# The first layer norm taken through a Toeplitz convolution: scaled transposed input, 1/std at the gate, mean and shift as a rank product

## The chip, the cores and the metric

The kernel runs on one core of a Trainium2 chip. The metric is the device time of one execution in microseconds (us), the median over several runs. A profiled execution on the same chip gives the trace from which all shares, durations and waits below are read.

Engines by the names of the profile: PE is TensorE (matmuls; PEld its weight loads), DVE is VectorE, ACT is ScalarE, POOL is GpSimd, SP is SyncE, whose queue issues nearly all DMAs here.

## The reference

One block of a network over x of shape (4, 1024, 2048) in fp32: an adaptive layer norm, a long convolution along the last axis, a gate, then a second adaptive layer norm, a feed-forward layer with a sum of low-rank updates, and a second gate.

```python
mod = (silu(c) @ wmod).reshape(4, 6, 1, 2048)
sa, ca, ga, sb, cb, gb = (mod[:, i] for i in range(6))
ga = (2 * (ga >= 0) - 1) * maximum(abs(ga), 0.25)        # gb likewise
h = layernorm(x) * (1 + ca) + sa
K = s4_kernel(...)                                        # 2048 taps, from small inputs
x = x + ga * (irfft(rfft(h, 4096) * rfft(K, 4096))[..., :2048] + D * h)
h = layernorm(x) * (1 + cb) + sb
x = x + gb * (h @ W.T + bias + sum_e w_e * (h @ A_e.T) @ Bf_e.T)
```

`layernorm` takes mean and variance over the 2048 columns. The convolution is causal and runs along the same 2048 columns that the norm runs over, with one kernel K for all rows. Both weights `ca`, `sa` depend on the batch entry (four of them) and the column.

## The kernel before, in words

**Tiles and stages.** The 4096 rows are 32 tiles of 128 rows, eight tiles to a batch entry. There are three stages. In the start, the modulation vectors come from 16 MB sections of `wmod` (tiles `wm`, 1 MB each; matmuls `modps`, line 317) and the convolution's taps are computed and laid out as Toeplitz blocks in a high and a low fp16 half (`kh`, `kl`, lines 233 to 287). Then comes the convolution of the 32 row tiles, and with it, as filler, the merging of the low-rank updates into W (`merge`, matmuls `lps`, line 486) and the three remaining sections of `wmod`. Last comes the feed-forward stage, 16 units of 256 rows by 2 column halves (`ffn_unit`, line 750), by a seven-product scheme.

**One row tile of the convolution.** `conv_load` (line 560) brings in x. `stats` (536) takes mean and variance with four `bn_stats` and one `bn_aggr`, and 1/std by a square root on ACT with a Newton step on DVE (`rstd`, 64). `normalize` (551) writes `n` = (x - mean)/std on DVE. `conv_prep` (565) transposes n, 16 blocks of 128x128, on PE into PSUM (`tp`, line 578), scales by 1 + ca and adds sa on ACT (line 582; both stand per partition once n is transposed), adds neighbouring column blocks to `sm` (590), and splits blocks and sums into fp16 high and low halves `hc`, `hs` (592, 593). `conv_mm` (596) multiplies these with the Toeplitz blocks: three families of matmuls, two column halves each, three products (high·high, high·low, low·high) per block pair, at line 614, into PSUM tiles `ya` and `yb`; the result is multiplied by the gate `gat` (633, 640), x is added and the row sums are kept (641). `conv_post` (654) stores the new x to `x1d` in HBM and takes the second norm's mean and 1/std into `ln2`.

**Scales.** The fp16 halves need bounded values. `fold_scale` (364) multiplies ca and sa by a power of two per batch entry, from the largest ca and sa over all partitions (`allmax`, line 58, one all-reduce over partitions on POOL); `gate_tile` (665) takes the scale out again.

**The two early rows.** Rows 0 and 1 (`EARLY`) are convolved in the start, before sa and the gate are known: their prep uses 1 + ca alone with a scale of its own (`early_scale`, 381). The convolution of the shift sa is made once with small matmuls (`shift_conv`, 390), stored to HBM, read back on all partitions and added (`shift_add`, 410); gate and x follow in `conv_late` (645).

**What sets the order.** The kernel's text says in which order work is issued; a scheduler then fixes every engine's queue before the run, by that order and by what is ready, as far as buffers allow. Each queue is worked through strictly in that order. Inside `conv_mm`, ten points (`tick`) call up the work of other rows after the strings of `PLAN` (line 812): P the second norm of the row before, N a piece of the next row's prep, S a piece of the filler, T the statistics of the row after next, F the first piece of that row's prep, L pieces of the feed-forward's left operands (last two rows). x has four buffers; PSUM has five banks for products (`acc`), two for transposes (`tps`), one for the modulation.

Of the kernel before, what the change touches and what calls it, by code (L numbers as in the profile page):

```python
# [26 lines left out]
NB = 4  # L27
# [7 lines left out]
class Net:  # L35
# [28 lines left out]
    def rstd(self, pool, var, out, n, name, scale=1.0):  # L64

        v = self.nc.vector
        ve = pool.tile([P, n], F32, tag=name + "_v", name=name + "_v")
        t = pool.tile([P, n], F32, tag=name + "_t", name=name + "_t")
        v.tensor_scalar(ve, var, 0.25 * scale, 0.25e-5, MUL, ADD)
        self.nc.scalar.activation(t, ve, AF.Sqrt)  # L70
        v.reciprocal(out, t)
        v.scalar_tensor_tensor(t, ve, out, t, MUL, ADD)
        v.reciprocal(out, t)
# [216 lines left out]
    def prep_mod(self, pool):  # L290
        nc, v = self.nc, self.nc.vector
        self.small = pool.tile([P, 265], F32, tag="small", name="small")
        nc.sync.dma_start(out=self.small, in_=self.io["small"])
        c = self.small[:, 201:265].rearrange("p (b j) -> p b j", j=16)
        th = pool.tile([P, NB, 16], F32, tag="mth", name="mth")
# [13 lines left out]
    def mod_load(self, pool, sec, j):  # L309
        w = pool.tile([P, D], F32, tag="wm", name="wm")  # L310
        src = self.io["wmod"].rearrange("(p j) n -> p j n", j=16)
        self.lastw = self.nc.sync.dma_start(out=w, in_=src[:, j, ds(sec * D, D)])
        return w
# [24 lines left out]
    def mod_gate(self, pool, name, bias=None):  # L338
# [10 lines left out]
        if bias is not None:  # L349
            bt = pool.tile([P, 512], F32, tag="mg2", name="mg2")  # L350
# [13 lines left out]
    def fold_scale(self, pool, mul, add, name, winv=None):  # L364
# [9 lines left out]
        self.hs, inv = s, _ = self.pow2(self.cst, self.allmax(pool, m, NB, name), NB, name)  # L374
# [6 lines left out]
    def early_scale(self, pool):  # L381
        v = self.nc.vector
        m = pool.tile([P, 1], F32, tag="esm", name="esm")
        v.tensor_reduce(m, self.ca[:, :, 0], AX.X, ALU.max, apply_absolute_value=True)
        v.tensor_scalar(m, m, LNMAX, None, MUL)
        self.es, self.einv = self.pow2(self.cst, self.allmax(pool, m, 1, "es"), 1, "es")
        self.cae = self.kpool.tile([P, NC], F32, tag="cae", name="cae")
        v.tensor_scalar(self.cae, self.ca[:, :, 0], self.es, None, MUL)

    def shift_conv(self, pool):  # L390

        nc, v = self.nc, self.nc.vector
        sa = pool.tile([P, NC], F32, tag="sae", name="sae")
        v.tensor_scalar(sa, self.sa[:, :, 0], self.es, self.hinv[:, 0:1], MUL, MUL)
        ps = self.tps.tile([P, NC], F32, tag="t", name="gsp")
        for m in range(NC):
            nc.tensor.matmul(
                ps[:, m:NC], self.kb[:, ds(P * m, P)], sa[:, 0 : NC - m],
                start=(m == 0), stop=(m == NC - 1), skip_group_check=True,
            )  # L400
        col = pool.tile([P, NC], F32, tag="gsc", name="gsc")
        v.tensor_copy(col, ps)
        pt = self.tps.tile([NC, P], F32, tag="t", name="gst")
        nc.tensor.transpose(pt, col, self.ident)
        row = pool.tile([NC, P], F32, tag="gsr", name="gsr")
        v.tensor_copy(row, pt)
        self.gsd = self.dram.tile([NC, P], F32, tag="gsd", name="gsd")
        nc.gpsimd.dma_start(out=self.gsd, in_=row)

    def shift_add(self, pool, ys):  # L410
        g = pool.tile([P, D], F32, tag="gat", name="gsb")
        self.nc.gpsimd.dma_start(out=g, in_=self.gsd.rearrange("c t -> (c t)").partition_broadcast(P))
        for y in ys:
            self.nc.vector.tensor_tensor(y, y, g, ADD)
# [121 lines left out]
    def stats(self, pl, x, tag):  # L536
        v = self.nc.vector
        st = pl["sm"].tile([P, 4, 6], F32, tag="st" + tag, name="st" + tag)
        for q in range(4):
            v.bn_stats(st[:, q], x[:, ds(512 * q, 512)])  # L540
        mv = pl["sm"].tile([P, 2], F32, tag="mv" + tag, name="mv" + tag)
        v.bn_aggr(mv, st)
        rs = pl["sm"].tile([P, 1], F32, tag="rs" + tag, name="rs" + tag)
        self.rstd(pl["sm"], mv[:, 1:2], rs, 1, "r" + tag)
        if tag in ACTNORM:
            mb = pl["sm"].tile([P, 1], F32, tag="mb" + tag, name="mb" + tag)
            v.scalar_tensor_tensor(mb, mv[:, 0:1], -1.0, rs, MUL, MUL)
            return mb, rs
        return mv, rs

    def normalize(self, pl, x, st, tag):
        n = pl["n"].tile([P, D], F32, tag="n", name="n" + tag)
        m, rs = st
        if tag in ACTNORM:
            self.nc.scalar.activation(n, x, AF.Identity, bias=m, scale=rs)
        else:
            self.nc.vector.tensor_scalar(n, x, m[:, 0:1], rs, SUB, MUL)
        return n

    def conv_load(self, pl, r):  # L560
        x = pl["x"].tile([P, D], F32, tag=f"x{r % 4}", name="x")
        self.nc.sync.dma_start(out=x, in_=self.io["x"][ds(P * r, P), :])
        return x

    def conv_prep(self, pl, r, x, st, out, shift=True):
        nc, v = self.nc, self.nc.vector
        b = r // 8
        n = self.normalize(pl, x, st, "1")
        yield

# [3 lines left out]
        for c0 in range(0, NC, 4):  # L574
            tp = self.tps.tile([P, 4, P], F32, tag="t", name="tp")
            t = pl["t"].tile([P, 4, P], F32, tag="t", name="t")
            for k in range(4):
                nc.tensor.transpose(tp[:, k], n[:, ds(P * (c0 + k), P)], self.ident)  # L578
            for k in range(4):
                c = c0 + k  # L580
                if shift:
                    nc.scalar.activation(  # L582
                        t[:, k], tp[:, k], AF.Identity,
                        bias=self.sa[:, c, b : b + 1], scale=self.ca[:, c, b : b + 1],
                    )
                else:
                    nc.scalar.activation(t[:, k], tp[:, k], AF.Copy, scale=self.cae[:, c : c + 1])
            tv = t.rearrange("p (i e) n -> p i e n", e=2)
            sm = pl["t"].tile([P, 2, P], F32, tag="sm", name="sm")
            v.tensor_tensor(sm, tv[:, :, 0, :], tv[:, :, 1, :], ADD)  # L590
            for (hi, lo), src, sl in ((hc, t, slice(c0, c0 + 4)), (hs, sm, slice(c0 // 2, c0 // 2 + 2))):
# [4 lines left out]
    def conv_mm(self, pl, hs, x, tick, early, pace):  # L596
# [4 lines left out]
        if not early:  # L601
            gv = self.gat.rearrange("p (j e t) -> p j e t", e=2, t=P)
        sums = pl["sm"].tile([P, 2], F32, tag="sums", name="sums")

        def family(ps, f, q, first):
            pf = ps.rearrange("p j t -> p (j t)")
            last = 4 * q + 3
            for i in range(last + 1):
                o = P * max(0, i - 4 * q)
                k0 = P * max(0, 4 * q - i)  # L610
                with pace(3 * (512 - o)):
                    for x, z in ((0, 0), (0, 1), (1, 0)):
# [5 lines left out]
                        first = False  # L618
                if i == 3 and q == 1:
                    tick()  # L620

        for q in range(2):
# [9 lines left out]
            if not early:  # L632
                v.tensor_tensor(yv[:, jj, 1, :], yv[:, jj, 1, :], gv[:, jj, 1, :], MUL)
# [5 lines left out]
            else:  # L639
                v.tensor_tensor(yv[:, jj, 0, :], pa, gv[:, jj, 0, :], MUL)  # L640
# [4 lines left out]
    def conv_late(self, x, y, sums, ratio):  # L645

        v = self.nc.vector
        for q in range(2):
            sl = ds(1024 * q, 1024)
            v.scalar_tensor_tensor(y[:, sl], y[:, sl], ratio, self.gat[:, sl], MUL, MUL)  # L650
# [3 lines left out]
    def conv_post(self, pl, r, x, y, sums):  # L654
        nc, v = self.nc, self.nc.vector
        STQ(nc).dma_start(out=self.x1d[r], in_=y)
        mn = pl["sm"].tile([P, 1], F32, tag="mn", name="mn")
        v.tensor_scalar(mn, sums[:, 0:1], sums[:, 1:2], -1.0 / D, ADD, MUL)
        sq = pl["sm"].tile([P, 1], F32, tag="sq", name="sq")
        nc.scalar.activation(x, y, AF.Square, bias=mn, accum_out=sq)  # L660
        rs = self.ln2[:, r, 1:2]
        self.rstd(pl["sm"], sq, rs, 1, "r2", 1.0 / D)
        v.tensor_tensor(self.ln2[:, r, 0:1], mn, rs, MUL)

    def gate_tile(self, pool, b):
# [3 lines left out]
        s = self.hinv[:, b : b + 1]  # L669
        if b == 0:  # L670
            for q in range(4):
# [3 lines left out]
                v.tensor_scalar(t[:, ds(512 * q, 512)], ps, s, self.kinv, MUL, MUL)  # L675
        else:
            nc.sync.dma_start(out=t, in_=self.gad[b].partition_broadcast(P))
            v.tensor_scalar(t, t, s, self.kinv, MUL, MUL)
# [133 lines left out]
PLAN = ("PNSL", "NL", "NSL", "NTL", "SL", "SL", "SL", "SL", "FSL", "SSL")  # L812
LPLAN = ("LL", "LL", "LL", "LL", "L", "0", "")
R0 = 5
WM, WMS = 3, 3
# [17 lines left out]
def net(ctx: ExitStack, tc: tile.TileContext, io):  # L833
# [5 lines left out]
    k.ln2 = k.const("ln2", [P, 32, 2])  # L839
    k.lfd = k.dram.tile([NU, 7, P, HC, 2, P], F16, tag="lfd", name="lfd")  # L840
# [10 lines left out]
    k.prep_mod(msm)  # L851

    def section(sec, pools):
# [5 lines left out]
        if sec == 0:  # L859
            k.sa = k.mod_column(msm, k.kpool, "sa", 0.0)  # L860
            k.hinv = k.fold_scale(msm, k.ca, k.sa, "fs1")
# [24 lines left out]
    for name, bufs in (("h", 2), ("n", 1), ("t", 2), ("y", EARLY), ("g", 1)):  # L886
        pl[name] = pool(left, "p1" + name, bufs)
    st = ExitStack()
    toe = k.toeplitz(pool(st, "st", 1, "right"))
    wms = pool(st, "wms", WMS, "right")  # L890
# [3 lines left out]
    xs, hs, sts, ys = {}, {}, {}, {}  # L894

    def prep(r, shift=True):
        return k.conv_prep(pl, r, xs[r], sts.pop(r), hs, shift)
# [4 lines left out]
    def load(r):  # L902
        if r < 4:
            with tc.issue_after(k.lastw.ins):
                xs[r] = k.conv_load(pl, r)
        else:
            xs[r] = k.conv_load(pl, r)

    def stats(r):
        sts[r] = k.stats(pl, xs[r], "1")  # L910

    n = 0
    for _ in section(1, (wms, wmp)):
# [6 lines left out]
    k.early_scale(msm)  # L920
    load(1)
    rows = (x for sec in (0, 2) for x in section(sec, (wms, wmp)))
    stats(0)
    take(prep(0, False), 9)
# [3 lines left out]
    take(prep(1, False), 9)  # L928
# [11 lines left out]
    def third():  # L940

        while not hasattr(k, "hinv"):
            yield
        k.shift_conv(msm)
        stats(2)
        yield from prep(2)

    ys[0] = k.conv_mm(pl, hs.pop(0), xs[0], lambda: None, True, pace)
    load(2)
    nxt = third()  # L950
    ys[1] = k.conv_mm(pl, hs.pop(1), xs[1], lambda: take(nxt, 1), True, pace)
# [3 lines left out]
    k.shift_add(pl["g"], [ys[r][0] for r in range(2)])  # L955
# [211 lines left out]
```

## Time and profile before

| what | value |
|---|---|
| median of 3 runs | 2142.18 us (2141.35 to 2144.37) |
| profiled execution, span | 2140.1 us, mean granted PE clock 0.988 |
| DMA | 484.11 MB, mean 226 GB/s; HBM read 326.94 MB, written 155.30 MB |
| first and last store of a finished convolution row | issued at 181.7 and 922.8 us |
| normalize (line 557, DVE) | 32 x 1340 ns |
| transposes of n (line 578, PE) | 512, mean 280 ns of one record |
| scale and shift (line 582, ACT) | 480 x 471 ns, from PSUM |
| split, high (592, ACT) and low (593, DVE), 128x512 | 128 x 640 ns and 128 x 684 ns |
| gate (633 and 640, DVE), 128x512 | 60 x 682 ns and 60 x 683 ns |
| POOL, whole run | 18 instructions, of which 5 all-reduces of 0.35 to 0.51 us |

The span is the time from the first to the last instruction of the one profiled execution; a stretch of it is named by its microseconds. A group's mean is the duration of one record, and records of one engine can overlap: matmuls follow each other faster than one of them takes from start to end. A row ends with the time that its engine sat idle just before the group, and with what ended most of that idle time.

### The profile page before, as it was taken

Reading aid. Unit: us, or ns where it says so; the run is one execution under the profiler, and the core shown is the slowest. Engines: PE = TensorE matmul, PEld = TensorE weight load, DVE = VectorE, ACT = ScalarE, POOL = GpSimd, SP = SyncE. Lnnn points to the kernel's source line nnn. Section 1 sums busy time; section 2 is a strip of 40 time slices with the busy share of each in tenths; the row PEclk is TensorE's granted clock in tenths of the full one; section 3 lists DMA queues with packets and bytes.
Section 4 is the critical chain, followed back from the end, with each engine's and each line's share of the span. In section 5 each row is a group of like instructions: output and inputs, shape, how many; then the busy total and the mean of one; then the engine's idle time right before and its main releaser. Section 6 shows DMA issues by size and latency. Waiting matters only on the chain.

```text
span 2140.1 us, 28438 instructions
## 1 busy us (share of the span) xinstructions
PE 2082.4 (97%) x11113; PEld 1026.1 (48%) x11113; DVE 1308.4 (61%) x2353; ACT 923.7 (43%) x1695; POOL 6.3 (0%) x18
## 2 busy tenths in 40 slices
PE   7898999999999999999999999999999999999998
PEld 2344455555555555554545545555444444444444
DVE  5439898898979999665565565575533323332323
ACT  1325876677767777745454555555200000000000
POOL 0000000000000000000000000000000000000000
PEclk7999999999999999999999999999999999999999
DMA  9977566787776554387564564564794645454542
GB/s 401 373 307 278 225 227 265 285 310 262 276 278 227 187 192 173 139 346 258 190 241 180 202 240 179 203 235 172 283 341 163 192 151 167 164 170 165 177 157 69
DMA packets 127236, 484.11 MB, mean 226 GB/s; under 512 B 13608, under 2 KB 13768, under 8 KB 95998
## 3 DMA queue, kind: packets, MB, share of 16 engines
q1 hardware_dynamic: 126192, 477.55, 61.4%
q10 hardware_dynamic: 526, 2.63, 0.4%
q8 instruction: 87, 1.43, 0.3%
q0 software_dynamic: 384, 2.11, 0.2%
q14 instruction: 47, 0.39, 0.0%
HBM read 326.94 MB, written 155.30 MB: 225 GB/s over the span
## 4 chain that ended last, share of the span: by engine, by line
PE 67%; DVE 18%; ACT 6%; DMA 5%; issue 2%; SPq 0%; ACTq 0%; POOL 0%; DVEq 0%; POOLq 0%
PE fZ L750 22%; PE fY L750 15%; PE fX L750 15%; PE ya L614 5%; PE yb L614 3%; PE tp L700 3%; DVE wch L514 2%; PE modps L317 2%; DVE st L540 2%; DVE hc L593 2%; DVE y L641 2%; ACT x L660 2%; DMA wcd<-wch 1%; ACT t L582 1%; PE lps L486 1%
## 5 line engine op out<-in xcount | busy, mean ns | idle before, releaser
L750 PEld LDWEIGHTS <-lf 128*128 128x128 f16 x5376 | 526.0, 98 | 620.9 <-issue 1.4
L750 PE MATMUL fZ<-w,lf 128*128 128x512 f16 x2304 | 513.6, 379 | 0.8 <-ACT p L758 0.8
L750 PE MATMUL fX<-w,lf 128*128 128x512 f16 x1536 | 342.8, 379 | 0.0
L750 PE MATMUL fY<-w,lf 128*128 128x512 f16 x1536 | 342.0, 379 | 0.0
L614 PEld LDWEIGHTS <-hc 128*128 128x128 f16 x2304 | 215.3, 98 | 204.6 <-issue 41.6
L768 DVE TENSOR_TENSOR xo<-xo,gb 128x512 f32<-128x512 f32 x128 | 87.8, 690 | 238.7 <-DMA xo<-x1d 227.2
L582 ACT ACTIVATE t<-tp,sa,ca 128x128 f32<-128x128 f32 x480 | 188.1, 471 | 21.6 <-PE tp L578 12.9
L614 PE MATMUL ya<-kh,hs 128*128 128x512 f16 (+3 forms) x768 | 193.7, 326 | 3.7 <-DVE kh L284 2.6
L614 PE MATMUL ya<-kh,hc 128*128 128x512 f16 (+3 forms) x768 | 192.7, 328 | 3.8 <-ACT qs L627 3.6
L614 PE MATMUL yb<-kh,hc 128*128 128x512 f16 (+3 forms) x768 | 192.2, 327 | 1.8 <-DVE y L640 1.4
L758 ACT COPY p<-fZ 128x512 f32<-128x512 f32 x64 | 37.2, 581 | 286.8 <-PE fZ L750 272.1
L614 PEld LDWEIGHTS <-hs 128*128 128x128 f16 x1152 | 105.9, 98 | 108.6 <-issue 28.4
L758 ACT COPY p<-fX 128x512 f32<-128x512 f32 x32 | 18.7, 585 | 316.3 <-PE fX L750 210.4
L702 ACT ACTIVATE gt<-tp,sb,cb 128x256 f32<-128x256 f32 x256 | 124.9, 576 | 60.8 <-PE tp L700 60.8
L317 PE MATMUL modps<-wm,sct 128*32 128x512 f32 x768 | 118.8, 662 | 14.1 <-DMA wm<-in_wmod 14.1
L614 PE MATMUL ya<-kl,hc 128*128 128x512 f16 (+3 forms) x384 | 125.8, 328 | 0.0
L614 PE MATMUL ya<-kl,hs 128*128 128x512 f16 (+3 forms) x384 | 125.1, 326 | 0.7 <-DVE kl L285 0.7
L614 PE MATMUL yb<-kl,hc 128*128 128x512 f16 (+3 forms) x384 | 125.6, 327 | 0.0
L773 DVE TENSOR_TENSOR fin<-fX,gb 128x512 f32<-128x512 f32 x32 | 22.1, 692 | 128.4 <-PE fX L750 128.3
L593 DVE TENSOR_TENSOR hc<-t,hc 128x512 f16<-128x512 f32 x128 | 87.5, 684 | 6.6 <-ACT hc L592 6.4
L486 PE MATMUL lps<-lbh,lac 128*128 128x512 f16 x256 | 86.3, 379 | 1.2 <-DVE we L488 1.2
L578 PE MATMUL tp<-ident,n 128*128 128x128 f32 x512 | 79.3, 280 | 8.1 <-ACT t L582 6.3
(264 smaller groups left out, 2228.0 us busy)
## 6 DMA issues: line engine op xcount, KB each, us to landing
wm<-in_wmod SPq DMA_DIRECT2D x96, 1024.0 KB
lfd<-lf SPq DMA_DIRECT2D x112, 512.0 KB
lf<-lfd SPq DMA_DIRECT2D x112, 512.0 KB
x<-in_x SPq DMA_DIRECT2D x32, 1024.0 KB
x1d<-y SPq DMA_DIRECT2D x32, 1024.0 KB
x<-x1d SPq DMA_DIRECT2D x32, 1024.0 KB
xo<-x1d SPq DMA_DIRECT2D x128, 256.0 KB
out<-xo SPq DMA_DIRECT2D x128, 256.0 KB
```

The lines of the kernel that those rows point to most:

```text
L317: self.last = self.nc.tensor.matmul(self.modps[32 * g : 32 * g + 32, :], self.sct[:, j].rearrange("p r b -> p (r b)"), w[:, ds(512 * g, 512)],
L486: nc.tensor.matmul(ps, la[:, x, k, h], y[:, k, osl], start=(n == 0), stop=(n == 5))
L514: v.tensor_tensor(hl[:, :, 1, :], tv, hl[:, :, 0, :], SUB)
L578: nc.tensor.transpose(tp[:, k], n[:, ds(P * (c0 + k), P)], self.ident)
L582: nc.scalar.activation(t[:, k], tp[:, k], AF.Identity, bias=self.sa[:, c, b : b + 1], scale=self.ca[:, c, b : b + 1],)
L593: v.tensor_tensor(lo[:, sl], src, hi[:, sl], SUB)
L614: nc.tensor.matmul(pf[:, o:512], h, self.kf[f][z][:, ds(k0, 512 - o)], start=first, stop=(i == last and (x, z) == (1, 0)), skip_group_chec ...
L700: nc.tensor.transpose(tp[:, c, r], xs[r][:, ds(P * (c0 + c), P)], self.ident)
L702: nc.scalar.activation(t[:, c0 + c], tp[:, c], AF.Identity, bias=self.sb[:, c0 + c, b : b + 1], scale=self.cb[:, c0 + c, b : b + 1],)
L750: nc.tensor.matmul(ps[name], lf[i][:, k, x, :], wc[i][k // 4][:, k % 4, y, :], start=(first and n == 0), stop=(n == 3 * HC - 1), skip_grou ...
L758: nc.scalar.copy(t, ps[name])
L768: v.tensor_tensor(x, x, self.gbias[:, h], ADD)
```

## The change

The norm is linear in x once mean and 1/std are known, and both are one number per row, while the convolution acts along the columns. The changed kernel uses that: with a row's mean m and standard deviation d, the convolution of (x - m)/d·(1 + ca) + sa is 1/d times [conv(x·(1 + ca)) - m·conv(1 + ca) + d·conv(sa)].

- **Input.** The host hands in x a second time, transposed by 128x128 blocks (`in_xT`, 1 MB per row tile). `conv_load` loads both. `normalize` and the 16 transposes per row are gone; `conv_prep` scales the transposed x in place on ACT by `cas` = (1 + ca)·s, now 8 blocks at a time, and sum and splits run on twice the width.
- **Scale.** The power of two s is made per row tile, from the largest of |m| + 46·d over the partitions and the largest |1 + ca| per batch entry (`scale_bound`, once): one all-reduce per row tile on POOL, with small operations on POOL (`g.`) and DVE around it.
- **Mean and shift.** `rank_rows` convolves -(1 + ca) and sa of all four batch entries once (8 vectors), splits them in three bf16 parts and stores them; `rank_load` brings them into `gm`, 72 of 128 partitions used, by 24 small DMAs on POOL. Each row's m·s and d·s are split in three bf16 parts as well, put into 18 columns of a 128x128 tile `spt`, transposed on PE (`svp`) and copied to bf16 (`sw`). One matmul of `sw` with `gm` per PSUM tile (`rank`) then adds mean and shift to the product.
- **Gate.** 1/std with the scale taken out (`rsx`, one number per row) is multiplied in at the gate, in a three-operand form.
- **Second norm.** `conv_post` keeps the sums of squares in `sqs` and makes 1/std for eight rows at once.
- **Order.** The prep of row r + 1 now starts and ends within row r's convolution (F is gone from `PLAN`); the transposed x has two buffers. In the start, `wm` takes turns over other free buffers: six at a time for the first section as before, five for the second and third.

The diff, cut to its core:

```diff
+    def scale_bound(self, pool):
+        m = pool.tile([P, NB], F32, tag="esm", name="esm")
+        v.tensor_reduce(m, self.ca.rearrange("p c b -> p b c"), AX.X, ALU.max, apply_absolute_value=True)
+        self.cmax = self.allmax(self.kpool, m, NB, "cmx")
...
+    def rank_load(self):
+        self.gm = self.kpool.tile([P, D], BF16, tag="gm", name="gm")
+        self.nc.gpsimd.memset(self.gm, 0.0)
+        for i in range(2 * NB):
+            src = self.gsd[i].rearrange("c j t -> j c t")
+            for k in range(3):
+                to = self.gm[ds(9 * i + 3 * k, 3)].rearrange("j (c t) -> j c t", t=P)
+                self.nc.gpsimd.dma_start(out=to, in_=src)
...
+    def stats(self, pl, r, x):
...
+        v.tensor_scalar(ve, mv[:, 1:2], 0.25, 0.25e-5, MUL, ADD)
+        nc.scalar.activation(t, ve, AF.Sqrt)
+        v.reciprocal(rs, t)
+        v.scalar_tensor_tensor(mv[:, 1:2], ve, rs, t, MUL, ADD)
+        v.reciprocal(rs, mv[:, 1:2])
+        g.tensor_scalar(am, mv[:, 0:1], -1.0, mv[:, 0:1], MUL, ALU.max)
+        g.tensor_scalar(am, mv[:, 1:2], LNMAX, am, MUL, ADD)
+        inv = self.allmax(pl["sm"], am, 1, "am1")
+        g.tensor_scalar(inv, inv, self.cmax[:, b : b + 1], 1e-18, MUL, ALU.max)
+        v.tensor_scalar(inv.bitcast(I32), inv.bitcast(I32), 0x7F800000, None, ALU.bitwise_and)
+        g.tensor_scalar(inv, inv, 1.0 / FP_TOP, None, MUL)
+        v.reciprocal(s, inv)
+        g.tensor_scalar(cas, self.ca[:, :, b], s, None, MUL)
+        g.tensor_scalar(rsx, rs, inv, None, MUL)
+        g.tensor_scalar(w, mv, s, None, MUL)
+        g.tensor_copy(h, w)
+        g.tensor_copy(sv[:, :, 0], h)
+        g.tensor_tensor(w, w, h, SUB)
+        g.tensor_copy(l, w)
+        g.tensor_copy(sv[:, :, 1], l)
+        g.tensor_tensor(sv[:, :, 2], w, l, SUB)
+        full = self.spt[r % 2]
+        if r % 8 < 2:
+            g.memset(full, 0.0)
+        g.tensor_copy(full[:, ds(18 * b, 18)].rearrange("p (a j) -> p a j", j=3), sp.unsqueeze(2).to_broadcast([P, 6, 3]))
+        tp = self.tps.tile([P, P], F32, tag="t", name="svp")
+        nc.tensor.transpose(tp, full, self.ident)
+        nc.scalar.copy(sw, tp)
+        return cas, rsx, sw
...
+        xt = pl["xt"].tile([P, NC, P], F32, tag="xt", name="xt")
+        self.nc.sync.dma_start(out=xt.rearrange("p c n -> p (c n)"), in_=self.io["xT"][r])
...
-        n = self.normalize(pl, x, st, "1")
...
-        for c0 in range(0, NC, 4):
...
-            for k in range(4):
-                nc.tensor.transpose(tp[:, k], n[:, ds(P * (c0 + k), P)], self.ident)
...
-                    nc.scalar.activation(
-                        t[:, k], tp[:, k], AF.Identity,
-                        bias=self.sa[:, c, b : b + 1], scale=self.ca[:, c, b : b + 1],
-                    )
...
+        for c0 in range(0, NC, HC):
+            t = xt[:, c0 : c0 + HC]
+            for k in range(HC):
+                nc.scalar.activation(t[:, k], t[:, k], AF.Copy, scale=cas[:, c0 + k : c0 + k + 1])
+            yield
...
+        def rank(ps, jj, e):
+            if not early:
+                nc.tensor.matmul(ps, st[2], mv[:, jj, e, :], start=False, stop=False, skip_group_check=True)
...
+                if i == 0 and f:
+                    rank(ps, slice(4 * q, 4 * q + 4), f // 2)
...
-                v.tensor_tensor(yv[:, jj, 1, :], yv[:, jj, 1, :], gv[:, jj, 1, :], MUL)
+                v.scalar_tensor_tensor(yv[:, jj, 1, :], yv[:, jj, 1, :], rsx, gv[:, jj, 1, :], MUL, MUL)
...
-        self.rstd(pl["sm"], sq, rs, 1, "r2", 1.0 / D)
-        v.tensor_tensor(self.ln2[:, r, 0:1], mn, rs, MUL)
+        nc.scalar.activation(x, y, AF.Square, bias=mn, accum_out=self.sqs[:, r : r + 1])
+        if r % 8 == 7:
+            sl = slice(r - 7, r + 1)
+            self.rstd(pl["sm"], self.sqs[:, sl], self.ln2[:, sl, 1], 8, "r2", 1.0 / D)
+            v.tensor_tensor(self.ln2[:, sl, 0], self.ln2[:, sl, 0], self.ln2[:, sl, 1], MUL)
...
-PLAN = ("PNSL", "NL", "NSL", "NTL", "SL", "SL", "SL", "SL", "FSL", "SSL")
+PLAN = ("PNSL", "NL", "NSL", "NTL", "SL", "SL", "SL", "SL", "SL", "SSL")
...
-WM, WMS = 3, 3
+WM = 3
...
+    r["xT"] = r["x"].reshape(32, P, NC, P).transpose(0, 3, 2, 1).reshape(32, P, D)
```

The early rows go the same way: `conv_late` adds the rank product with four matmuls and four additions per row, and `shift_conv` and `shift_add` are gone.

## The prediction

> **What bounds the kernel now.** First the page: engines, then the slices, then the costliest groups.
>
> ```profile
> PE 2082.4 (97%) x11113; PEld 1026.1 (48%) x11113; DVE 1308.4 (61%) x2353; ACT 923.7 (43%) x1695; POOL 6.3 (0%) x18
> ...
> PE   7898999999999999999999999999999999999998
> ...
> DVE  5439898898979999665565565575533323332323
> ...
> L578 PE MATMUL tp<-ident,n 128*128 128x128 f32 x512 | 79.3, 280 | 8.1 <-ACT t L582 6.3
> ```
>
> TensorE (PE) is busy in every slice, VectorE (DVE) close behind in the first 17, GpSimd (POOL) is empty. The busy times by stretch, cut at the first gated rows (175) and at the last convolution eviction (926), columns PE, PEld, DVE, ACT, POOL, granted clock, DMA share, GB/s:
>
> ```profile
> 0.00:175.00 175.00, 140.99 (x776) 55.75 (x776) 84.61 (x226) 38.10 (x97) 5.42 (x16) 0.86 0.90 360
> 175.00:926.00 751.00, 734.46 (x4520) 394.22 (x4519) 668.05 (x1410) 539.85 (x1099) 0.92 (x2) 1.00 0.65 238
> 926.00:2140.00 1214.00, 1206.94 (x5821) 576.11 (x5818) 555.78 (x719) 345.73 (x501) 0.00 (x0) 1.00 0.57 200
> ```
>
> The start is paced by DMA (0.90 of the engines), the convolution stage and the feed-forward stage by PE: 16.5 us of 751 and 7 of 1214 are idle. So a change in the convolution is worth what it does to PE's queue there, and the 1214 us stay.
>
> **PE, removed and added.** PE's timeline around one group of four transposes:
>
> ```profile
> 573.93 0.22 PE L614 MATMUL yb<-kh,hc 128*128 128x128 f16 x1
> 573.99 0.61 PE L578 MATMUL tp<-ident,n 128*128 128x128 f32 x4
> 574.43 0.38 PE L614 MATMUL ya<-kh,hc 128*128 128x512 f16 x1
> ```
>
> From the start of the four to the next matmul is 0.44 us, 0.11 each, not the 0.28 of a single record. Sixteen per row over the 30 rows of the stage: 480 x 0.11 = -52.8 us. The two early rows' 32 lie in the DMA-paced start and count nothing. Added per row: four rank matmuls of 512 columns; matmuls of that width follow each other in 0.216 us (559.85 to 560.07 in the same timeline), so 30 x 4 x 0.216 = +25.9; and one transpose for the statistics, 29 x 0.11 = +3.2. Net -24 us. Of the 8.1 us that PE waited at L578, I credit 7.
>
> **DVE, ACT, DMA: nothing on the path.** DVE loses the normalize (32 x 1.34 us) and most of the second norm's small chain (five operations, 0.15 + 0.16 + 0.22 + 0.16 + 0.16 us per row, now once in eight rows), and gains two short ones per row; the gate as a three-operand form costs 0.74 (L488, PSUM) against 0.68. It was 89% busy under PE's 98%, and only falls. ACT's scalings read SBUF instead of PSUM: between 0.39 (L587) and 0.47 (L582), 72% busy before. Were DVE's cover gone, its own total, about 600 us, still lies under PE's. DMA gains 32 x 1.05 MB behind each x load in SP's queue: 30 of them, 31 MB, over some 740 us add 43 GB/s to 238, share 0.65 to 0.77, less than the 0.90 that the start carried at 360. In the start the extra loads of rows 0 and 1 cost 2.1 MB / 0.36 = 5.8 us, less the 1 MB broadcast that goes, up to 11 if rows 2 and 3 collide too: +5. The 24 small DMAs on POOL (0.54 to 0.83 us each by its own DMA rows, 13 to 20 us) lie between the rank rows (gsd at 118 us) and the gate matmuls (169 us): covered. Late by over 30 us they would hold row 0's late add, and PE behind it.
>
> **POOL, which the page shows empty.** Per row it gets 14 tiny operations, an all-reduce, and hops to DVE and back, all before the scaled x can be made (ACT waits for cas) and before PE may transpose the statistics (svp waits for spt). In the built program's order the all-reduce and the ordinary operations come from two code libraries, and each alternation has a reload in front: 71 reloads, two per row, against two in all before. What one costs, POOL's timeline shows once:
>
> ```profile
> 0.86 0.20 POOL masks.py:197 MEMSET ident<- 128x128 f32 x1
> 10.59 0.28 POOL L237 TENSOR_SCALAR_AFFINE_SELECT rev<-rev 128x128 f32<-128x128 f32 x1 [9.52 <-issue]
> ```
>
> and the rows of line 237 name it:
>
> ```profile
> L237 POOLq MODIFY_POOL_CONFIG  x2: 11/11/11, 1.1 to 1.1; - x2
> ```
>
> 9.5 us with nothing to wait for. The second reload (config at 12.2, next instruction at 39.88) hid in a wait for DVE: anything from 0 to 27.6. I take 9.0, by the row at 9.5, shaded since DMA was saturated then; bounds 0 and 13 (half as much again as taken). The all-reduce itself takes 0.4; small operations 0.10 (128x1 memset) to 0.28 (affine select), taken 0.2.
>
> [...]
>
> Throughput alone would do: 2 x 9 + 0.4 + 3 = 21.4 us of POOL per row, against 25 us per row now (751/30). But the order is greedy. At rows 4, 12, 17, 22 and 27 three or four rows' all-reduces stand ahead of the first row's cas and spt, as each hop to DVE lets the next row's all-reduce slip in; and svp stands at a fixed place in PE's queue, with the next rows' convolution matmuls behind it. So per row: PE's work in the built order from the statistics' first POOL operation to svp (columns at the pitches above), times 1.05 (751 us for 716 of such work now), against reloads x 9 + all-reduces x 0.4 + small operations x 0.2. Where a later row's chain is the tighter start, it is taken. PE available / needed / stall:
> row 3, 16.2 / 2 reloads, 13 operations, 21.0 / 5; row 4, 37.6 / 8, 27, 79.0 / 41; row 8, 16.4 / 2, 13, 21.0 / 5; row 9 (from row 10's start), 14.9 / 2, 15, 21.4 / 6; row 12, 39.8 / 6, 28, 60.8 / 21; row 16, 17.8 / 2, 13, 21.0 / 3; row 17 (from 18's), 37.2 / 6, 26, 60.4 / 23; row 20, 31.6 / 4, 18, 40.4 / 9; row 22 (from 23's), 31.5 / 6, 26, 60.4 / 29; row 25 (from 26's), 14.8 / 2, 13, 21.0 / 6; row 27, 25.7 / 8, 27, 79.0 / 53; row 31, 15.7 / 2, 13, 21.0 / 5. The other rows fit. Sum +207 us; 50 reloads stand in it, so each us of price moves it by 50.
>
> After the stall rows 12, 17 and 22 have still to be prepared: 8 scalings x 0.39, sum 0.68, casts 1.05 and 0.64, remainder 0.68 = 6.2 us before PE's first matmul, x 3 = +19. Behind a stalled svp everything waits that PE feeds: DVE's and ACT's evictions, the merges, SP's stores.
>
> Sum: -24 - 7 + 207 + 19 + 5 = +200 on the span of 2140.1; the median of the runs stands 2.1 above the span: 2342 us, +9%.
>
> [...]
>
> **Rivals.** (a) Reloads cost half the row, 4.75 us: the stalls at rows 4, 12, 17, 22, 27 shrink to 15, 10, 4, 10, 19 = 59, the others vanish, and the total is 2142 - 31 + 59 + 19 + 5 = 2194. For it: the one row is the program's first load under saturated DMA. Against: DMA is at 0.65 in the stage too, and the gap has no other owner. (b) Faster: the reloads are free, as the second one may have been, running ahead in POOL's idle time, and the late preparation hides as well; then only PE's books count, 2142 - 31 + 5 = 2116. It decides where stalls and preparation together stay under 26 us, that is a reload under about 1 us. Against: the reload stands behind the row's own first operations in POOL's queue, so it can't start before them. (c) Dearer, 13 us, with 410 us of stall (207 + 4 x 50, two rows more): 2142 - 31 + 410 + 19 + 5 = 2545; POOL then needs 29 us per row and is the bound everywhere.
>
> **Chances.** Main 0.52 (price 8 to 10.5: 2290 to 2420), (a) 0.26 (2150 to 2290), (c) 0.08, (b) 0.10, and 0.04 that gain and stalls nearly cancel. The range takes main and (a) with most of (c)'s near side: 2160 to 2460. Under 0.2% (4 us) can't be told from no change. Faster 0.10 (b), same 0.03, slower 0.87.
>
> **What would show it.** Right: POOL gaps of some 9 us of "issue" before each all-reduce and the first small operation after it; PE idle put down to svp, some 200 us, in five large holes; DVE and ACT waiting on POOL for the bitwise step and cas; transposes gone from PE; feed-forward still 1214 us. Wrong: those gaps near 1 us, or PE idle under 30 us in the stage; or holes put down to SP's loads, so that DMA was the price.

## The result and the profile after

The changed kernel takes 2421.74 us (2417.46 to 2423.54), the kernel before 2141.76 us beside it: ratio 1.1305, 95% interval 1.1286 to 1.1325. The forecast was 2342 us, in a range of 2160 to 2460. The profiled execution spans 2415.7 us, 275.6 more than before's 2140.1, at a mean granted clock of 0.928.

The page after, engines and slices:

```profile
PE 2101.3 (87%) x10761; PEld 997.7 (41%) x10761; DVE 1262.8 (52%) x2053; ACT 894.1 (37%) x1571; POOL 180.6 (7%) x529
...
PE   6688488785796867837999999999999999999999
...
POOL 1130111112101111111000000000000000000000
PEclk7797689997897988969999999999999999999999
```

PE, full in nearly every slice before, has holes through the first 19, and the granted clock falls in the same slices. POOL is in work there, yet at 7% of the span: its busy time does not show what it costs.

To place the loss, both spans are cut where the first gated row's `ya` eviction starts and where the last one starts (line 640 before, 672 after): start, convolution stage, rest. Busy times by stretch, before (columns PE, PEld, DVE, ACT, POOL, clock, DMA share, GB/s):

```profile
189.50:920.90 731.40, 714.86 (x4406) 383.10 (x4404) 650.99 (x1375) 526.68 (x1074) 0.92 (x2) 1.00 0.65 238
920.90:2140.10 1219.20, 1212.04 (x5848) 578.96 (x5846) 558.34 (x726) 348.40 (x504) 0.00 (x0) 1.00 0.57 201
```

and after:

```profile
227.00:1194.50 967.50, 726.21 (x4067) 364.77 (x4065) 614.55 (x1102) 504.50 (x977) 140.88 (x437) 0.87 0.54 199
1194.50:2415.70 1221.20, 1213.47 (x5855) 579.52 (x5852) 558.32 (x728) 349.35 (x504) 0.00 (x0) 1.00 0.58 201
```

The start grew by 37.5 us (189.5 to 227.0), the stage by 236.1, the rest by 2.0: 275.6 together. In the stage PE idles 241.3 us (967.5 less 726.2) where it idled 16.5, and its fewer matmuls take 11 us more. DMA fell to 0.54 busy: no engine is full, and DMA is not. PE's waits over the whole span (us, times, longest):

```profile
PE svp L590 <- POOL spt L588: 161.5, 25, 28.7
PE modps L319 <- DMA wm<-in_wmod: 61.6, 23, 13.4
PE ya L644 <- ACT hs L616: 53.3, 3, 38.8
```

The first and the third hang on POOL: `svp` waits for `spt`, and `hs` for ACT, which itself waited 133.9 us for `cas` from POOL. Of the second, 27.9 us lie in the start and 33.7 in the stage. In e1 below, where POOL's small operations are gone, the stage's part falls to 0.2 us and the start's stays (30.5), so only the stage's part is POOL's. There SP issues the loads of `wm` late: some when PE had at last read the buffer, the longest wait (13.4 us, at 733) behind a store in SP's queue that waited for DVE, which had itself stood 4.4 us for POOL. POOL's own queue:

```profile
POOL am_r L60 <- issue: 194.0, 28, 10.3
...
POOL am_r L569 <- issue: 77.9, 9, 10.4
POOL am_r L571 <- issue: 67.9, 8, 11.4
POOL cas L574 <- issue: 59.3, 7, 10.0
POOL am L565 <- issue: 47.3, 5, 10.9
```

Before an all-reduce (L60) POOL stands still for 6.9 us in the mean, waiting for nothing, and before the first ordinary operation behind it for 8.7 (these four lines and 18.5 us, 2 times, at L566: 270.9 us over 31). Those are the reloads, by the trace a pair of `MODIFY_POOL_CONFIG` rows each (71 in all): 15.6 us for one each way. One batch on POOL's timeline shows how they stack up:

```profile
543.39 0.41 POOL L60 PARTITION_ALL_REDUCE am_r<-am  x1 [5.79 <-issue]
551.38 0.26 POOL L571 TENSOR_SCALAR am_r<-am_r 128x1 f32<-128x1 f32 x1 [7.58 <-issue]
551.74 0.30 POOL L569 TENSOR_SCALAR am_r<-am_r,cmx_r 128x1 f32<-128x1 f32 x1
552.14 0.29 POOL L565 TENSOR_SCALAR am<-mv 128x1 f32<-128x1 f32 x1
...
561.16 0.41 POOL L60 PARTITION_ALL_REDUCE am_r<-am  x1 [5.95 <-issue]
568.53 0.34 POOL L574 TENSOR_SCALAR cas<-ca,s 128x16 f32<-128x16 f32 x1 [6.96 <-issue]
```

Line 571 at 551.38 is the step behind one row's bitwise operation. Between it and that row's `cas` at 568.53 the queue puts operations of other rows and an all-reduce, with two reloads. PE's timeline, at four of its largest waits:

```profile
302.62 0.61 PE L644 MATMUL ya<-kh,hs 128*128 128x512 f16 x1 [14.04 <-ACT hs L616]
...
573.99 0.47 PE L590 MATMUL svp<-ident,spt 128*128 128x128 f32 x1 [21.06 <-POOL spt L588]
...
916.40 0.47 PE L590 MATMUL svp<-ident,spt 128*128 128x128 f32 x1 [28.73 <-POOL spt L588]
...
1077.31 0.61 PE L644 MATMUL ya<-kh,hs 128*128 128x512 f16 x1 [38.81 <-ACT hs L616]
```

The second and third are the 13th and 23rd `svp`, rows 12 and 22, where the prediction's table had stalls of 21 and 29. The first and last stand just ahead of the 5th and 28th `svp`, rows 4 and 27, where it had 41 and 53; they are waits at `hs`, behind a late `cas`. Row 17's `svp` waits 9.3 us where the table had 23, with the 13.4 us at `modps` ahead of it.

### The profile page after: what moved, and what is told of

Same layout as the page of the kernel before. It is cut to its first block, busy times and chain, and to the rows that moved or that the text cites. A ratio compares the mean times of both kernels' runs of the same rounds, so it can differ in the third digit from the quotient of the medians.

```text
span 2415.7 us, 28160 instructions
## 1 busy us (share of the span) xinstructions
PE 2101.3 (87%) x10761; PEld 997.7 (41%) x10761; DVE 1262.8 (52%) x2053; ACT 894.1 (37%) x1571; POOL 180.6 (7%) x529
## 4 chain that ended last, share of the span: by engine, by line
PE 63%; issue 13%; DVE 8%; DMA 7%; ACT 5%; POOL 4%; SPq 0%; POOLq 0%; ACTq 0%; DVEq 0%
PE fZ L786 20%; PE fX L786 13%; PE fY L786 13%; PE ya L644 6%; PE yb L644 4%; PE tp L736 2%; PE modps L319 2%; DMA wm<-in_wmod 2%; ACT xt L610 2%; PE lps L497 2%; DVE st L555 1%; DVE wch L525 1%; DMA x<-in_x 1%; DMA we<-in_WT 1%; DMA lws<-in_coeffs 1%
## 5 line engine op out<-in xcount | busy, mean ns | idle before, releaser
L644 PE MATMUL ya<-kh,hs 128*128 128x512 f16 (+3 forms) x768 | 197.0, 336 | 53.4 <-ACT hs L616 53.3
L644 PE MATMUL yb<-kh,hc 128*128 128x512 f16 (+3 forms) x768 | 212.4, 341 | 4.4 <-DVE we L499 4.4
L610 ACT ACTIVATE xt<-xt,cas 128x128 f32<-128x128 f32 x512 | 160.7, 394 | 133.9 <-POOL cas L574 133.9
L644 PE MATMUL ya<-kh,hc 128*128 128x512 f16 (+3 forms) x768 | 204.1, 330 | 5.9 <-ACT qs L659 5.8
L319 PE MATMUL modps<-wm,sct 128*32 128x512 f32 x768 | 135.1, 748 | 63.2 <-DMA wm<-in_wmod 61.6
L590 PE MATMUL svp<-ident,spt 128*128 128x128 f32 x32 | 13.9, 434 | 163.7 <-POOL spt L588 161.5
L644 PE MATMUL yb<-kl,hc 128*128 128x512 f16 (+3 forms) x384 | 130.6, 340 | 0.0
L555 DVE BATCH_NORM_STATS2 st<-x 128x6 f32<-128x512 f32 x128 | 82.5, 683 | 19.7 <-DMA x<-in_x 19.7
```

The costliest lines, as they stand in the source:

```text
L319: self.last = self.nc.tensor.matmul(self.modps[32 * g : 32 * g + 32, :], self.sct[:, j].rearrange("p r b -> p (r b)"), w[:, ds(512 * g, 512)],
L610: nc.scalar.activation(t[:, k], t[:, k], AF.Copy, scale=cas[:, c0 + k : c0 + k + 1])
L644: nc.tensor.matmul(pf[:, o:512], h, self.kf[f][z][:, ds(k0, 512 - o)], start=first, stop=(i == last and (x, z) == (1, 0)), skip_group_chec ...
```

## The experiments

Times are medians in us. "Start" is where the first gated row's `ya` eviction begins, "stage" lasts to the last one's start, "idle" is the stage less PE's busy time in it.

| kernel | time | ratio to before | start | stage | idle |
|---|---|---|---|---|---|
| before | 2142 | 1 | 189.5 | 731.4 | 16.5 |
| after | 2421.7 | 1.1305 | 227.0 | 967.5 | 241.3 |
| e1 small operations on DVE | 2149.1 | 1.0033 (1.0021 to 1.0045) | 203.4 | 721.0 | 29.5 |
| e2 no all-reduce | 2232.7 | 1.0421 (1.0402 to 1.0441) | 224.7 | 789.6 | 73.2 |
| e3 row by row | 2334.6 | 1.0898 (1.0880 to 1.0915) | 231.0 | 882.8 | 143.2 |
| e4 before with reloads | 2152.4 | 1.0050 (1.0036 to 1.0064) | 193.1 | 735.6 | 19.8 |
| e5 = e1, svp late | 2140.7 | 0.9986 (0.9976 to 0.9996) | 199.1 | 720.8 | 25.8 |
| e6 = after, svp late | 2388.8 | 1.1139 (1.1124 to 1.1155) | 222.6 | 945.4 | 217.3 |
| e7 = e3, svp late | 2320.0 | 1.0826 (1.0805 to 1.0847) | 223.5 | 870.6 | 144.0 |
| e8 = e5, no rank matmuls | 2121.0 | 0.9890 (0.9877 to 0.9904) | 199.7 | 701.4 | 36.3 |
| e9 = e2, svp late | 2180.9 | 1.0177 (1.0160 to 1.0194) | 217.0 | 742.4 | 45.9 |
| e10 = e5, DVE trimmed | 2140.5 | 0.9998 (0.9988 to 1.0008) | 198.1 | 720.4 | 27.3 |
| e11 before, e10's order | 2141.5 | 0.9994 (0.9984 to 1.0003) | 184.3 | 736.6 | 19.7 |
| e12 = e5, long rank rows | 2120.9 | 0.9898 (0.9882 to 0.9915) | 184.5 | 718.9 | 23.0 |

The reload counts in the expectations are two too high each. By the trace, where each reload is a pair of `MODIFY_POOL_CONFIG` rows, after, e3, e6 and e7 have 71, e1 2, e2 9, e4 66, before 2.

**e1: the small operations leave POOL.** In `stats`, all 14 of these lines:

```diff
-        g.tensor_scalar(am, mv[:, 0:1], -1.0, mv[:, 0:1], MUL, ALU.max)
+        v.tensor_scalar(am, mv[:, 0:1], -1.0, mv[:, 0:1], MUL, ALU.max)
```

> The changed kernel with the 14 small operations per row moved from POOL to DVE; the all-reduce alone stays on POOL, so that its library stays loaded (4 reloads in the whole program instead of 71). Theory (reloads in POOL's queue are the price): the convolution stage, 988 us now, loses the 215 us of PE waits at svp, ya and modps behind them, the start most of its 37 us, and the total lands at 2105 to 2150 (2142 - 24 - 7 + 5 = 2116 by the prediction's own books, plus whatever DVE's 32 x 14 x 0.2 = 90 us more of work costs). Rival 1 (the chain's length and hops between engines, with or without reloads): over 2250, svp still waits over 80 us. Rival 2 (the 34 MB of transposed x): over 2250, with modps or the scalings waiting for DMA.

2149.1, at the upper edge of what the theory gave. One edit takes 273 of the 280 us away, so the loss is in POOL's chain, and the transposed x, still loaded in full, is not it. PE still waits 28.6 us at `svp`, for DVE now.

**e2: the small operations stay, the reloads go.**

```diff
-        inv = self.allmax(pl["sm"], am, 1, "am1")
+        inv = T(1, "inv1")
+        g.tensor_copy(inv, am)
```

> The changed kernel with the rows' all-reduce replaced by a POOL copy of each partition's own bound: the maximum over the partitions is left out, all small operations stay on POOL. 11 reloads instead of 71, 14 small operations and the hops to DVE and back stay. Theory: 2105 to 2150, svp waits under 15 us. Rival 1 (small POOL operations and hops): over 2250. Rival 2 (DMA): over 2250.

2232.7, neither: 189 us of the loss go with the reloads, 84 more than in e1 stay. PE's waits in the stage, and one of them:

```profile
PE svp L591 <- POOL spt L589: 50.6, 15, 5.0
...
454.21 0.47 PE L591 MATMUL svp<-ident,spt 128*128 128x128 f32 x1 [4.32 <-POOL spt L589]
```

No hole is over 5 us; a chain of 14 short operations with hops to DVE simply ends later than its place in PE's queue. So this POOL chain costs PE 50.6 us with hardly a reload left.

**e3: row by row.** POOL's operations of a row are held behind the last one (`spt`) of the row before:

```diff
+        if r > 2:
+            hold.enter_context(self.tc.issue_after(self.lastspt.ins))
...
-        g.tensor_copy(full[:, ds(18 * b, 18)]...
+        self.lastspt = g.tensor_copy(full[:, ds(18 * b, 18)]...
```

> The changed kernel with each row's POOL chain held behind the chain of the row before it: the same two reloads per row (73 in all), but no batches of three or four rows. Theory: a row's chain is then two reloads (6 + 10), the all-reduce and the small work, some 22 us, against 24 us of PE per row; the large holes go and 2150 to 2260 is left. Rival (the reloads' sum counts, whatever their order; or they hurt others by their traffic): within 30 us of 2422.

2334.6, in neither range: the batches are worth 85 us of the stage (967.5 to 882.8), far less than the theory gave them.

**e4: reloads that nobody waits for,** in the kernel before:

```diff
+        dm = pl["sm"].tile([P, 1], F32, tag="dm", name="dm")
+        self.nc.gpsimd.tensor_scalar(dm, mv[:, 0:1], -1.0, mv[:, 0:1], MUL, ALU.max)
+        self.allmax(pl["sm"], dm, 1, "dm")
```

> The kernel before, with a small POOL operation and a dummy all-reduce of the row's mean added to every row, whose results nobody reads: 68 reloads. Theory (a reload costs only who waits for POOL's queue): 2142 within 6 us. Rival (the reloads' code traffic, or POOL's port, slows DMA, PE or DVE): 2170 or more.

2152.4, 0.5% slower: a small miss, 4 us in the stage and 4 in the start for 64 more reloads. Here a reload's price is nearly all in who stands behind it.

**e5 to e7: svp later.** The transpose moves out of `stats` into a function of its own, called in the middle of the convolution one row later (a "U" in `PLAN`):

```diff
-PLAN = ("PNSL", "NL", "NSL", "NTL", "SL", "SL", "SL", "SL", "SL", "SSL")
+PLAN = ("PNSL", "NL", "NSL", "NTL", "SL", "USL", "SL", "SL", "SL", "SSL")
...
+                elif a == "U" and r + 1 < 32:
+                    turn(r + 1)
```

> The small operations on DVE as in the run before, and the transpose of a row's statistics (svp) half a convolution to a whole one later in PE's queue, just ahead of the row that uses it. Theory: the 28.6 us that PE waited at svp in 19 short waits were the latency of a chain through a busy DVE, and go: 2149 - 28 = 2121, between 2112 and 2135, faster than the kernel before. Rival (DVE, 87% busy in the stage, is by now a second bound): 2137 to 2150, the waits come back at hs, yb or lps.

2140.7, the rival's number. The waits at `svp` are gone, and the stage is as long as in e1 (720.8 to 721.0): 14.1 us now stand at `qs`, ACT's copy of one product, which comes late. PE's books are near the prediction, 695.0 us busy, 19.9 less than before:

```profile
199.10:919.90 720.80, 694.96 (x4090) 355.08 (x4088) 647.59 (x1493) 492.26 (x957) 14.72 (x36) 0.99 0.73 272
```

> The changed kernel as it is (small operations on POOL, batches, 73 reloads), with svp later in PE's queue. Theory (POOL's queue with its reloads is late for both of its products, the transposed statistics and cas): the 160 us at svp shrink, but cas stays late behind the batches of three and four all-reduces, so ACT's scalings and PE's first matmuls of a row (hs) wait in its place: 2230 to 2350. Rival (only the place of svp in PE's queue was wrong): under 2180.

2388.8, over the theory's range, but its mechanism: `svp` falls from 161.5 to 95.6 us and `hs`, behind `cas`, rises from 53.3 to 85.3. The two products of the chain are late together.

> Row by row as in e3, with svp later: all reloads are there (73), none is in the way of PE if a row's chain (two reloads, 16 us, the all-reduce, 14 small operations, two hops to DVE) keeps inside the 24 us that PE takes per row. Theory: 2145 to 2210. Rival (POOL is full at 29 us per row, as the 883 us of the stage in e3 might say): 2300 or more.

2320.0: the rival holds. POOL's waits in e7's stage:

```profile
POOL am_r L572 <- issue: 231.3, 28, 12.7
POOL am_r L60 <- issue: 207.5, 28, 10.6
POOL am L569 <- DVE mv L562: 120.2, 10, 22.7
POOL am L568 <- DVE mv L557: 21.7, 5, 10.4
```

Of 871 us, 446 are reloads (6.9 at `cas` included), 173 busy, and 146 a wait inside the chain: its first operation needs only the mean, its second the standard deviation, and POOL is held between them (120.2, and 25.3 in three rows that name other releasers at L569). Only 21.7 us are spent waiting for a next row's mean. Per chain, of 29: 15.4 + 6.0 + 5.0 = 26 us, over the 24 that PE needs for a row. So POOL's chain, with the wait inside it, sets the pace, at 20% busy. That wait is not POOL's own work: in the longest one (22.7 us, to 862.8) the root on ACT and the step behind it on DVE were made only at 855.3 and 862.4, behind other work in their queues, with the variance at hand since 840.

> The kernel of e5 without the four rank matmuls per row in rows 2 to 31: the mean and the shift are left out of those rows. Theory (PE is the bound again): 120 x 0.216 = 26 us less than e5. Rival (DVE is the bound): within 8 us of e5.

19.7 us less than e5, nearer to PE's bound than to DVE's: PE's busy time falls by 29.9 and 10.5 come back as idle.

**e9: e2 with svp late.**

> The kernel of e2 (the rows' maximum over the partitions left out, small operations on POOL, few reloads) with svp later in PE's queue. Theory: e2's 69 us over e5 in the convolution stage are PE waiting 2 to 5 us at svp for POOL's chain of small operations, and the lower granted clock (0.96) that follows such holes; with svp late the stage falls from 790 to 720 to 740 and the whole to 2155 to 2185, the start's 21 us of reloads staying. Rival (POOL's small operations are late for cas too, or slow DVE down): the waits move to hs and qs, 2205 or more.

2180.9, as the theory said (the stage 2 us past its range). `svp` falls from 50.6 to 3.5 us in the stage, the granted clock rises from 0.96 to 0.99, the stage loses 47 us. With the reloads there, the same edit brought 22 (e6).

**e10 and e11: trimming, and its control.** e10 puts `cas` and two copies on ACT, drops one, gives `qs` priority and loads row 3 later; e11 has the last two edits in the kernel before.

```diff
-            self.lasta = nc.scalar.copy(qs, pa)
+            with self.tc.high_priority():
+                self.lasta = nc.scalar.copy(qs, pa)
...
-    load(3)
     take(rows, 40)
+    load(3)
```

> The kernel of e5 with four of the row's small operations taken from DVE (cas and two copies on ACT, one copy dropped), qs's copy with priority in ACT's queue, and the loads of row 3 behind the modulation weights in the start. Theory (in e5 DVE at 90% and ACT's order hold PE for the 26 us that it idles in the stage; four extra loads hold the start by 10 us): 2118 to 2134. Rival (both are noise of the order, the gain is eaten again): 2138 to 2146.

> A control: the kernel before with the same two edits of order (qs's copy with priority, row 3's load behind the modulation weights). Theory: its PE waited 3.6 us at qs and its start held 1 MB per row, so 2134 to 2143. Rival (these edits, not the change, make e10 fast): as far below 2142 as e10 is below 2141.

Both stay where their base was (2140.5, 2141.5). 11 us of DVE time less in the stage brought nothing, so DVE's load is not what holds e5; PE still waits 17.9 us at `qs`, and what makes `qs` late was not found. e11's start came 5.2 us sooner (184.3) and its stage took 5.2 us longer.

**e12: the rank rows in long pieces.** In e5 the start is 9.6 us later than before. The DMA rate falls while the 24 small loads of `gm` lie there (busy times by stretch, the last two columns the DMA share and GB/s):

```profile
0.00:120.00 120.00, 92.36 (x531) 32.42 (x531) 67.10 (x221) 34.21 (x81) 9.12 (x23) 0.89 0.99 405
120.00:140.00 20.00, 14.59 (x84) 3.92 (x84) 2.29 (x3) 1.42 (x3) 12.94 (x22) 0.91 1.04 295
```

```diff
-        self.gsd = self.dram.tile([n, NC, 3, P], BF16, tag="gsd", name="gsd")
-        nc.gpsimd.dma_start(out=self.gsd.rearrange("i c j t -> (i c) j t"), in_=g3)
+        self.gsd = self.dram.tile([3, n, NC, P], BF16, tag="gsd", name="gsd")
+        for j in range(3):
+            nc.gpsimd.dma_start(out=self.gsd[j].rearrange("i c t -> (i c) t"), in_=g3[:, j])
...
-            src = self.gsd[i].rearrange("c j t -> j c t")
+            src = self.gsd[:, i].rearrange("j c t -> j (c t)")
...
-                to = self.gm[ds(9 * i + 3 * k, 3)].rearrange("j (c t) -> j c t", t=P)
-                self.nc.gpsimd.dma_start(out=to, in_=src)
+                self.nc.gpsimd.dma_start(out=self.gm[ds(9 * i + 3 * k, 3)], in_=src)
```

> The kernel of e5 with the rank rows' 24 small DMAs (12 KB each, in pieces of 256 bytes) reading and writing whole rows of 4 KB instead; the row layout in DRAM is changed for it, the work is the same. Theory: in e5's trace the DMA rate falls from some 420 to some 275 GB/s for the 28 us in which these 24 lie, with the DMA engines still shown over 0.9 busy, 4 MB or 9.6 us of weights lost, which is all of the 9.6 us by which e5's first gated row is later than before's; so the rate stays over 380 there, the first gated row starts by 192 and the whole is 2128 to 2135, faster than the kernel before. Rival (the start is held by the four megabytes of transposed x, or by the DMAs' number): start at 197 to 200, 2138 to 2143.

2120.9, better than the theory gave, 1.0% faster than the kernel before and the fastest that computes the whole. The rate in e12's same stretch:

```profile
120.00:140.00 20.00, 17.60 (x114) 5.56 (x110) 3.12 (x4) 3.67 (x8) 12.19 (x24) 1.00 1.02 388
```

93 GB/s more over 20 us are 1.9 MB, 4.6 us at the 405 GB/s ahead of it. The start gained 14.6. The rest goes with the queue: the scheduler now puts the early rows' rank products ahead of filler matmuls that wait for weights. In e5 they stood behind them,

```profile
174.25 1.93 PE L319 MATMUL modps<-wm,sct 128*32 128x512 f32 x8 [3.18 <-DMA wm<-in_wmod]
...
181.02 0.61 PE L688 MATMUL rkq<-gm,sw 128*128 128x512 bf16 x1
```

and in e12 they are done before the gate is:

```profile
150.14 1.03 PE L688 MATMUL rkq<-gm,sw 128*128 128x512 bf16 x4
```

How the 10 us split between this order and the DMAs that followed was not tried.

## Why the prediction was right, and where not

The direction and the place were right, and the sum of +200 us on the span has the form that the trace has. The forecast is 76 us short, and where its largest term agrees, that is in part luck (below). Term by term:

| term | predicted | measured | from |
|---|---|---|---|
| PE's matmuls and transposes | -24 | -19.9 | busy 714.9 before, 695.0 in e5 |
| PE idle in the stage (tp, stalls, late prep) | -7 + 207 + 19 | +224.8 | 241.3 against 16.5 |
| lower clock in the stage | no term | +31.2 | busy 726.2 after, 695.0 in e5 |
| start | +5 | +37.5 | 227.0 against 189.5 |
| rest | 0 | +2.0 | 1221.2 against 1219.2 |

The measured terms sum to 275.6, the forecast to 200: the difference is mainly the start (32) and the clock (31). The clock's part is a difference between two kernels with nearly the same matmuls, not a separate measurement.

**PE's books held,** 0.11 a transpose and 0.216 a rank matmul: e8 takes 29.9 us of busy time away where the prediction's 25.9 stood. That PE's 7 us at `tp` would be gained did not: in e5 its idle time is 25.8 against 16.5, moved to `qs`. Of the 31 us promised on PE, 10.6 arrive in e5's stage.

**The stalls: right in sum, only partly for the reason given.** A pair of reloads took 15.6 us, not 18, and the holes at rows 12 and 22 came as the table had them, those at rows 4 and 27 shorter (14 and 39 against 41 and 53) and at `hs`, not at `svp`. At `svp` PE idles 133.9 us in the stage, not some 200; 53.3 at `hs` and 33.7 at `modps` fill the sum up, which is in part luck. And "the other rows fit" was wrong: rows 11 and 15 wait 7.8 and 5.8 us at `svp`. The step "21.4 us of POOL per row, against 25" failed: e7, with no batch and nobody queued early, needs 26 per chain, since the small operations took 0.27 to 0.65 us in the mean instead of 0.2, the all-reduce 0.77 instead of 0.4, and since the wait for the standard deviation sits inside the chain. And the table asked only whether POOL had the time, not where `svp` stands. Undone one after the other, the stage's 246.7 us over e5 are 178 for the reloads (after to e2; 85 of them for the batches, by e3), 47 for `svp`'s place behind a reload-free chain (e2 to e9) and 22 for the rest of POOL's chain (e9 to e5). The parts depend on the order in which they are undone: `svp`'s place is worth 22 in the full kernel.

**Rival (b) was mispriced.** It gave 2116 for free reloads. With 9 reloads left of 71, e2 takes 2232.7 and e9 2180.9; 2116 needs the small operations off POOL and the start mended (e12, 2120.9). Rival (a)'s stalls do not follow from the table as printed: its entries at 4.75 us a reload give 7, 0, 0, 3 and 19, not 15, 10, 4, 10 and 19, unless a tighter start applies that the table does not show.

**The start: +5 was far too little, and "24 small DMAs, covered" was wrong.** What the extra loads cost by themselves stays open, as no run leaves them out: e12 has them all and starts 5 us before the kernel before, but the 1 MB broadcast of the shift is gone there and `wm` uses other buffers. What stands behind the 37.5, undone in turn: 2.3 from after to e2, 21.3 from e2 to e1 (PE's wait at `svp` in the start falls from 27.6 to 7.9; e2's POOL has reload gaps of 11.4 and 8.1 us in the first rows' chain), 4.3 for `svp` of rows 0 and 1 ahead of `modps` (e1 to e5), 14.6 for the small DMAs and the order that they set (e5 to e12), less 5.0.

**The clock** has no term in the forecast's sum. Nearly the same matmuls take 726.2 us at a granted 0.87 in the stage after and 695.0 at 0.99 in e5, 31.2 us less. The trace after shows where it falls: in the hole of 38.8 us that ends at 1077.3 the granted clock is 1.00 until 1041.5, 0.50 from there on, and 1.00 again only at 1082.5, 5.2 us after PE has work again. In those 5.2 us matmuls of 512 columns follow each other in 0.42 us (1081.40 to 1081.82), behind them in 0.22 (1082.59 to 1082.81). In slices of half a us the stage after has 17 stretches with a clock under 0.75, and PE is busy for 85.1 us in them (3.5 before); half of that, an estimate of 43 us, is more than the 31.2. In e2 the matmuls of the stage take 19.9 us longer than in e9 (716.5 to 696.5, clock 0.96 to 0.99).

**DMA in the stage and the other engines** went as said: DVE's total fell (1308.4 to 1262.8), the transposed x is hidden (e1, 2149.1 with all of it), the feed-forward stayed (1219.2 and 1221.2).

## What to carry to other kernels

Count how often a queue changes between two kinds of operation before putting both on it, and look in the trace for what a change costs. Here POOL's busy share stayed at 7% of the span while a change, of which there were 71, stood for some 6 to 11 us ahead of all that followed, and the scheduler batched the rows so that each paid for its neighbours (85 us of the stage, after to e3). A consumer at a fixed place in the bound engine's queue waited here for a whole chain (`svp`: 47 us of the stage, e2 to e9), so place it late by what the chain takes, waits on third engines included. And when such a chain is mended, look at the small transfers beside a DMA that is nearly full (0.99 busy in e5's first 120 us): here they, and the order that came with them, held the change's whole remaining gain (2140.7 to 2120.9).

## What the runs showed of the hardware

The two directions of a reload differ: in the changed kernel 6.9 us in the mean to the all-reduce, 8.7 back, up to 11.4. And a reload at the start of an execution seems to depend on what POOL ran last in the one before. The prediction read its price off POOL's first affine select, 9.52 us of "issue" before it; in the changed kernel the same operation has no such gap,

```profile
1.37 0.29 POOL L238 TENSOR_SCALAR_AFFINE_SELECT rev<-rev 128x128 f32<-128x128 f32 x1 [0.29 <-POOL ident masks.py:197]
```

while in e1 it has:

```profile
10.40 0.28 POOL L238 TENSOR_SCALAR_AFFINE_SELECT rev<-rev 128x128 f32<-128x128 f32 x1 [9.32 <-issue]
```

Eight profiles show the same: before and e1, e4, e5 and e12 end with an all-reduce on POOL and have 9.26 to 9.67 us there; after and e2 and e3 end with an ordinary operation and have 0.29. So the row that gave the price was most likely a reload back, left by the execution before.

Short DMAs slowed a full DMA here without showing it in its share: at 1.04 (e5) against 1.02 (e12) of the engines the rate was 295 against 388 GB/s, for 24 loads of 12 KB in pieces of 256 bytes beside 1 MB loads. The profile counts as many packets under 512 bytes in e12 as in e5 (14832 and 14800), so what about the short pieces slows the rest stays open.
